# A decoder layer on one core: attention scores from float32r parts, whole-row moves of the values, expert rows by token

## The chip, the cores and the metric

The kernel runs on one core of a Trainium2 chip. It is one launch. The metric is the device time of that launch in microseconds (us). The kernel before takes 2743.19 us (median of three runs, 2734.66 to 2744.45). One further execution was profiled; its trace is what the text reads.

Five engines work side by side, each through its own queue in order: PE (TensorE, matrix products), DVE (VectorE), ACT (ScalarE), POOL (GpSimd) and SP (SyncE, which here issues every DMA). PEld is PE's loading of the stationary operand.

## The reference, cut to what matters

All is float32. There are B = 32 sequences of L = 256 tokens and D = 256 channels. Each passes three blocks, and each block ends in `x = layernorm(x + block(x))`:

```python
# 1. state-space block: d_inner 512, 16 states, chunks of 64 tokens
xc, res = split(x @ W_in.T + b_in); u = silu(causal_conv3(xc))
dlt, Bm, Cm = split(u @ W_x.T);     delta = softplus(dlt @ W_dt.T + b_dt)
h[t] = exp(delta[t] * A) * h[t-1] + delta[t] * Bm[t] * u[t]   # from zero in each chunk
y = sum_n(h * Cm) * silu(res);      block = y @ W_out.T + b_out
# 2. cross-attention: 16 heads of 16 channels, 256 keys from ctx
block = softmax(q @ k.T / 4) @ v  -> @ w_o.T + b_o
# 3. eight experts, FF = 704; tokens 32e .. 32e+31 of a sequence belong to expert e
block = (silu(x @ w1[e]) * (x @ w3[e])) @ w2[e]
```

## The kernel before, in words

**The state-space block** sets the rhythm. A step covers 32 of the 512 inner channels of one sequence, so there are 16 steps to a sequence and 512 in all (`STEPS`). In a step, SP loads delta and delta*u with every row repeated for eight states (`ld`), ACT takes four exponentials (`da`, L573), DVE makes `bu` (L602) and runs the recurrence as one scan over 1024 elements (L621), POOL multiplies by C (L637), and after every fourth step PE sums over the states (`y`, L651) and DVE gates the sum (`yg`, L667). The loads run three steps ahead (`AHEAD`). Both `bu` and B (`b_bc`) lie in PSUM.

**Attention** of a sequence follows its last step: the product with `w_out`, residual and layernorm, transposes, the product with `w_q` (`queries`, L789). Keys and values are made ahead (`keys_ahead`, L691) and kept in DRAM. Queries and keys go through DRAM as well, and come back by `spread_heads` (L678) with the 16 channels of a head at partitions 0 to 15 or 64 to 79 of `qT` and `kT`; the rest of these 64-row halves is zero. `scores` (L809) makes two heads at a time, one in each 64-row half: four float32 matmuls of 256 columns, a group. A head's scores are made twice. `maxima` (L825) makes them with queries along the partitions, and DVE reduces each head to its row maxima (`tops`, L838). The negative maxima are transposed on PE (L844), copied by ACT (L847), written to DRAM and loaded into row 63 and row 127 of `qT`; the same rows of `kT` are ones. `attns` (L874) then makes the scores with keys along the partitions, so that the maximum is already subtracted; ACT takes the exponentials (`es`, L894) and PE multiplies by the values (L863). Values lie as `v[P, 2, H, 32]`: 16 channels of a head, a one (for the sum of the softmax) and 15 zeros. They are loaded by two DMAs in pieces of 16 elements. `finish` (L924) divides, multiplies by `w_o` and applies the second layernorm; the result goes to DRAM (`x2d`).

**Experts** come in 32 units. The first 24 take 256 rows of one expert from eight sequences. The last eight, for sequences 24 to 31, take 128 rows of each of two experts from four sequences; four of them need sequence 31. A unit loads its rows (`load_xe`, L1070, through `rows_of`, L1065), transposes them, runs w1, w3 and w2 (L1133, L1197, L1212), adds and normalizes, and stores to `out`.

**The order of the work** is written by a planner at build time. Each part is a generator (a chain) that says when it could go on and on which engine; `in_order` (L80) always takes the chain that can start first, by a clock of assumed costs (`spend`; `MM`, `EV`, `VE`, `GP` from L307). It assumes that a DMA lands 3.5 us after its issue (`LANDING`). What a chain issues is then fixed in the engines' queues; on the chip every instruction waits for what it needs. PSUM gives five banks to all products (`RING`); `take` reserves banks and `done` returns them.

```python
        ss = [bank("s").rearrange("p (t n) -> p t n", t=2) for _ in heads]
        for t in range(2):
            for h, s in zip(heads, ss):
                g, r = h // 2, HR * (h % 2)
                nc.tensor.matmul(s[:, t, :], left[r : r + n, g, t * P : (t + 1) * P],
                                 right[r : r + n, g, :], start=True, stop=True)
        return ss, spend("PE", 2 * MM + 0.2)
```

## Time and profile before

| what | value |
|---|---|
| median of three runs | 2743.19 us |
| the profiled execution, its own time | 2743.78 us |
| its span, first to last instruction | 2742.0 us |
| first `bu` of the scans starts | 42.59 us |
| last scan ends | 2513.4 us |
| mean granted TensorE clock | 0.959 |
| DMA | 505.86 MB in 491497 packets, 177204 of them under 512 B |
| `v<-v_all` issue time on SP, min / median / max | 543 / 1177 / 3422 ns |

The profile's page gives the busy time of each engine, a row of tenths over 40 equal slices of the span, the DMA queues, the chain of work that ended last, and the costliest groups of instructions: line, engine, operation, `out<-in`, shapes, count, then busy time, mean duration in ns, idle time of the engine just before them and what ended it. A float32 matmul leaves two records, so 1024 matmuls appear as x2048. The view by windows gives the busy time of each engine in a stretch of the span. The view of waits tells which engine waited for which. The timeline tells the instructions in order, with the idle time before one and its releaser in brackets.

### The profile page before, as it was taken

The page shows a single profiled execution, that of the slowest core. Times are in us where ns is not written, and L with a number is a line of the kernel's source. Part 1 is how long each engine was busy: PE and PEld are TensorE (multiplying, and loading weights), DVE is VectorE, ACT ScalarE, POOL GpSimd, SP SyncE. Part 2 cuts the span into 40 slices and gives each one's busy share as a digit, 9 for nine tenths or more (in the row PEclk, how much of TensorE's full clock was granted, in tenths as well). Part 3 has the DMA queues.
Part 4 walks back from the last instruction along what each step waited for, and adds up shares of the span by engine and source line. Part 5 has one row for each costly group of instructions (what it writes and reads, how often), then busy time and mean ns, then how long its engine had stood idle before and what let it go on. Part 6 is the DMA issues. An engine that isn't in the chain of part 4 may idle for free.

```text
span 2742.0 us, 48659 instructions
## 1 busy us (share of the span) xinstructions
PE 2466.3 (90%) x16964; PEld 1705.3 (62%) x16964; DVE 2380.6 (87%) x2413; ACT 2043.4 (75%) x4327; POOL 1643.7 (60%) x1145
## 2 busy tenths in 40 slices
PE   5788989889899899989998989999999899998988
PEld 4565666566566666666666666665666566666767
DVE  4999999999999999999999999999999899896212
ACT  6887888888778878887878778888788788674331
POOL 4775766666666666575666665666666666553000
PEclk8899999999999999998999999999999999999999
DMA  7866666666676666676666666667666566666464
GB/s 203 228 199 176 193 187 181 189 191 191 187 199 186 181 167 190 176 197 177 167 198 187 198 175 186 187 177 195 190 197 179 163 172 180 185 174 181 150 195 144
DMA packets 491497, 505.86 MB, mean 184 GB/s; under 512 B 177204, under 2 KB 339252, under 8 KB 491252
## 3 DMA queue, kind: packets, MB, share of 16 engines
q1 hardware_dynamic: 491252, 502.75, 64.8%
q8 instruction: 135, 2.21, 0.4%
q14 instruction: 110, 0.90, 0.1%
HBM read 426.07 MB, written 76.55 MB: 183 GB/s over the span
## 4 chain that ended last, share of the span: by engine, by line
PE 29%; DVE 11%; ACT 8%; DMA 5%; issue 3%; POOL 1%; SPq 1%; DVEq 0%; ACTq 0%; POOLq 0%
PE ps_h L1133 8%; PE s L816 6%; DVE h L621 5%; PE ps_down L1212 4%; ACT da L573 3%; PE y L651 3%; DVE bu L602 2%; DVE tops L838 2%; PE ps_in L349 2%; PE ps_oT L863 2%; DMA ld<-dd 1%; DMA xe<-x2d 1%; PE ps_out L349 1%; PE ps_qk L349 1%; ACT es L894 1%
## 5 line engine op out<-in xcount | busy, mean ns | idle before, releaser
L637 POOL TENSOR_TENSOR h<-h,c_bc 128x1024 f32<-128x1024 f32 x512 | 1209.1, 2362 | 740.6 <-DVE h L621 627.0
L621 DVE TENSOR_TENSOR_SCAN h<-da,bu 128x1024 f32<-128x1024 f32 x512 | 1168.9, 2283 | 50.4 <-ACT da L573 5.8
L573 ACT ACTIVATE da<-ld,a_neg 128x252 f32<-128x252 f32 x2048 | 864.6, 504 | 188.3 <-DVE h L621 138.4
L602 DVE TENSOR_TENSOR bu<-ld,b_bc 128x1024 f32<-128x1024 f32 x512 | 626.1, 1223 | 19.9 <-DMA ld<-dd 8.0
L816 PE MATMUL s<-kT,qT 63*128 63x256 f32 x2048 | 345.4, 416 | 45.6 <-DVE tops L838 22.8
L894 ACT ACTIVATE es<-s 128x512 f32<-128x512 f32 x512 | 277.9, 594 | 140.6 <-PE s L816 75.9
L838 DVE TENSOR_REDUCE tops<-s 128x2 f32<-128x512 f32 x512 | 325.2, 677 | 41.6 <-PE s L816 41.1
L1133 PE MATMUL ps_h<-x2T,w 128*128 128x256 f32 (+2 forms) x1536 | 343.5, 368 | 9.5 <-ACT es L894 1.7
L816 PE MATMUL s<-qT,kT 64*128 64x256 f32 x2048 | 313.8, 405 | 22.5 <-DMA qT<-tops 13.0
L651 PE MATMUL y<-h,sel_y 128*32 128x256 f32 x4096 | 280.8, 397 | 52.3 <-POOL h L637 36.9
L816 PEld LDWEIGHTS s<-kT,qT 63*128 63x128 f32 x2048 | 213.8, 193 | 151.9 <-DVE tops L838 50.8
L1133 PEld LDWEIGHTS ps_h<-x2T,w 128*128 128x128 f32 (+1 forms) x1536 | 246.7, 186 | 89.7 <-issue 35.1
L349 PE MATMUL ps_in<-xT,w_in 128*128 128x256 f32 x1024 | 258.4, 397 | 8.7 <-ACT da L573 2.6
L816 PEld LDWEIGHTS s<-qT,kT 64*128 64x128 f32 x2048 | 200.9, 189 | 102.3 <-issue 39.6
L651 PEld LDWEIGHTS y<-h,sel_y 128*32 128x32 f32 x4096 | 131.8, 113 | 177.4 <-POOL h L637 55.1
L349 PEld LDWEIGHTS ps_in<-xT,w_in 128*128 128x128 f32 x1024 | 192.8, 196 | 60.4 <-issue 12.9
L420 POOL TENSOR_TENSOR u<-u,shifted 128x512 f32<-128x512 f32 x128 | 151.4, 1183 | 39.7 <-ACT u L407 34.7
L323 POOL TENSOR_SCALAR ln_rstd<-ln_mv 128x2 f32<-128x2 f32 x96 | 20.9, 218 | 254.2 <-DVE ln_mv L320 250.0
L407 ACT ACTIVATE shifted<-ps_in,tap_b,conv_w 128x256 f32<-128x256 f32 x256 | 130.8, 567 | 22.5 <-PE ps_in L349 10.9
L863 PE MATMUL ps_oT<-es,v 128*32 128x256 f32 x2048 | 142.4, 391 | 3.7 <-DVE h L1197 1.2
L349 PE MATMUL ps_out<-w_out,yg 128*128 128x256 f32 x512 | 117.6, 383 | 0.4 <-DVE yg L667 0.4
L375 ACT ACT_TABLE_LOAD x90 | 115.5, 1283 | 1.4
(135 smaller groups left out, 2987.5 us busy)
## 6 DMA issues: line engine op xcount, KB each, us to landing
ld<-dd SPq DMA_DIRECT2D x1024, 256.0 KB
w<-in_w SPq DMA_DIRECT2D x128, 352.0 KB
x<-in_x SPq DMA_DIRECT2D x64, 256.0 KB
dd<-delta SPq DMA_DIRECT2D x32, 512.0 KB
dd<-u SPq DMA_DIRECT2D x32, 512.0 KB
w<-in_w SPq DMA_DIRECT2D x32, 384.0 KB
w13y<-in_w SPq DMA_DIRECT2D x32, 352.0 KB
c_bc<-bcd SPq DMA_DIRECT2D x64, 128.0 KB
```

What stands on the lines that cost most here:

```text
L349: nc.tensor.matmul(ps[:, j, :], l, r, start=(k == 0), stop=(k == len(terms) - 1))
L420: nc.gpsimd.tensor_tensor(u[:, cc], u[:, cc], at, ALU.add)
L573: nc.scalar.activation(da[:, g, q].rearrange("p (k t) -> p k t", t=CHUNK)[:, :, 1:], loads[i][:, 0, g].rearrange("p (k t) -> p k t", t=CHU ...
L602: nc.vector.tensor_tensor(bu, loads[i][:, 1].unsqueeze(2).to_broadcast([P, GB, NQ, L]), b_bc.unsqueeze(1).to_broadcast([P, GB, NQ, L]), AL ...
L621: nc.vector.tensor_tensor_scan(h.rearrange("p g q t -> p (g q t)"), das_of.pop(i).rearrange("p g q t -> p (g q t)"), bu.rearrange("p g q t ...
L637: nc.gpsimd.tensor_tensor(hs[i], hs[i], c_bc, ALU.mult)
L651: nc.tensor.matmul(y[32 * j : 32 * j + 32, :], sel_y[:, g, :], hs[i - NJ + 1 + j][:, g, q, :], start=(g == 0 and q == 0), stop=(g == GB - ...
L816: nc.tensor.matmul(s[:, t, :], left[r : r + n, g, t * P : (t + 1) * P], right[r : r + n, g, :], start=True, stop=True,)
L838: nc.vector.tensor_reduce(top[:, h % 2, h // 2, :], s, AX.X, ALU.max)
L863: nc.tensor.matmul(oT[32 * j : 32 * j + 32, :], v[:, k, 4 * g + j, :], ess[j][:, k, :], start=(k == 0), stop=(k == 1), tile_position=(0, 3 ...
L894: nc.scalar.activation(es, s, AF.Exp, scale=1.0 / DK**0.5)
L1133: nc.tensor.matmul(ps[:m, i, :], w_tiles[u, which, e][k][:, f * P : f * P + m], right, start=(k == 0), stop=(k == 1),)
```

## The change

1. **Scores.** `qT` and `kT` become float32r. Queries and keys are split on POOL into a float32r copy (`hi`) and the rest (`lo = full - hi`): `parts_of`, two POOL instructions of 128x512 and two stores to DRAM for every sequence's queries and again for its keys. The 64 rows of a head now hold all four products: `qT` has (part, channel) with each row twice in a row, `kT` has (channel, part) and that twice over. `qT` comes by DMAs in which the repeat is an inner dimension of the source, 256 KB each in place of 64 KB, still four to a sequence; `kT` by eight DMAs of 128 KB in place of four of 64 KB.
2. **Maxima.** They don't go through DRAM any more. Two small POOL instructions split them into parts in `padded`, PE makes two 128x128 transposes in place of one, ACT writes the negative to `mTs`. In `attns`, each score matmul is followed by a second one that adds the maximum (`pick` picks the head's two rows): 1024 matmuls more.
3. **Values.** A row in DRAM holds 17 elements to a head, the ones with them, and `v` is loaded by one DMA of whole rows of 288 elements.
4. **Experts' rows.** `rows_of` puts the 32 tokens outside and the four sequences inside: the DMAs for `xe` and for `out` go from 4x32x256 to 32x4x256.
5. **Setup.** The weights and biases of q and k are put into the new column order by eight POOL copies; their bias loads are sixteen DMAs in place of eight.
6. **The planner's costs**: some are changed, and a group of scores is now put at 0.4 (maxima) or 0.7 in place of 1.14.

```diff
+F32R = mybir.dt.float32r
+DV = DK + 1
+VW = (H - 1) * DV + 32 + 1
-    k_all = dram.tile([B, D, L], F32, name="k_all")
-    v_all = dram.tile([B, L, D], F32, name="v_all")
+    k_all = dram.tile([B, DK, 2, 2 * NG, 2, L], F32, name="k_all")
+    v_all = dram.tile([B, L, VW], F32, name="v_all")
...
+        def ordered():
+            for k in range(2):
+                for i in range(2):
+                    at = slice(i * P, (i + 1) * P)
+                    nc.gpsimd.tensor_copy(
+                        w[:, k, at].rearrange("p (c j g) -> p g j c", j=2, c=DK),
+                        raw[:, k, at].rearrange("p (g j c) -> p g j c", j=2, c=DK),
+                    )
+            spend("POOL", 1.6)
...
-    kT = keep.tile([P, HG, L], F32, name="kT")
...
-    qT = keep.tile([P, HG, L], F32, name="qT")
-    nc.gpsimd.memset(qT, 0.0)
+    kT = keep.tile([P, HG, L], F32R, name="kT")
+    qT = keep.tile([P, HG, L], F32R, name="qT")
+    mTs = [keep.tile([P, L], F32R, name=f"mT_{i}") for i in range(2)]
+    padded = keep.tile([P, 2, 2, HR], F32R, name="padded")
+    pick = keep.tile([P, HG], F32R, name="pick")
...
-    MM = 0.47
-    EV = {1: 0.47, 2: 0.6, 4: 1.06}
-    VE = {1: 0.41, 2: 0.69, 4: 1.23}
-    GP = {1: 0.7, 2: 1.27, 4: 2.36}
+    MM = 0.49
+    EV = {1: 0.42, 2: 0.56, 4: 1.05}
+    VE = {1: 0.41, 2: 0.66, 4: 1.225}
+    GP = {1: 0.7, 2: 1.23, 4: 2.36}
...
+    def parts_of(n, b, full, t, d):
+
+        hi = unit1.tile([P, 2, L], F32R, tag="hi", name=f"{n}_hi_{b}")
+        lo = full.bitcast(F32R)
+        yield t, "POOL"
+        nc.gpsimd.tensor_copy(hi, full)
+        nc.gpsimd.tensor_tensor(lo, full, hi.bitcast(F32), ALU.subtract)
+        t = spend("POOL", 2 * GP[2])
+        yield t, "SP"
+        for s, part in enumerate((hi, lo)):
+            part = part.bitcast(F32)
+            if n == "q":
+                dma(d[:, s].rearrange("i c x t -> (c x) i t"), part)
+            else:
+                at = d[:, s].rearrange("c x i t -> c x (i t)")
+                dma(at, part.rearrange("p i t -> p (i t)"))
...
             for j in range(2):
-                src = d.rearrange("(i g j c) t -> i j c g t", i=2, j=2, c=DK)[half, j]
-                dma(dst[HR * j : HR * j + DK, 4 * half : 4 * half + 4, :], src)
+                at = dst[HR * j : HR * (j + 1), NG * half : NG * (half + 1), :].bitcast(F32)
+                if dst is qT:
+                    src = d[half, :, :, NG * j : NG * (j + 1)]
+                    src = src.rearrange("s c g t -> (s c) (g t)").unsqueeze(1)
+                    at = at.rearrange("p g t -> p (g t)")
+                    dma(at, src.to_broadcast([2 * DK, 2, NG * L]))
+                else:
+                    src = d[:, :, NG * j : NG * (j + 1), half].rearrange("c s g t -> (c s) g t")
+                    for s in range(2):
+                        dma(at[2 * DK * s : 2 * DK * (s + 1)], src)
...
-            for t in range(2):
-                src = v_all[b, t * P : (t + 1) * P].rearrange("p (h d) -> p h d", d=DK)
-                dma(v[:, t, :, :DK], src)
+            dma(v, v_all[b].rearrange("(t p) c -> p t c", p=P))
...
-    def scores(heads, left, right, n):
+    def scores(heads, left, right, lowered):
...
                 nc.tensor.matmul(
                     s[:, t, :],
-                    left[r : r + n, g, t * P : (t + 1) * P],
-                    right[r : r + n, g, :],
+                    left[r : r + HR, g, t * P : (t + 1) * P],
+                    right[r : r + HR, g, :],
                     start=True,
-                    stop=True,
+                    stop=not lowered,
                 )
-        return ss, spend("PE", 2 * MM + 0.2)
+            for h, s in zip(heads, ss):
+                g, r = h // 2, HR * (h % 2)
+                if lowered:
+                    nc.tensor.matmul(
+                        s[:, t, :],
+                        pick[r : r + HR, g : g + 1].to_broadcast([HR, P]),
+                        mTs[g // NG][r : r + HR, :],
+                        start=False,
+                        stop=True,
+                    )
+        return ss, spend("PE", 0.7 if lowered else 0.4)
...
-            nc.tensor.transpose(ps, top.rearrange("p j g t -> p (j g t)"), ident)
-            yield spend("PE", 0.2), "ACT"
-            rows = unit2.tile([H, P], F32, tag="rows", name="rows")
-            nc.scalar.activation(rows, ps, AF.Identity, scale=-1.0)
...
-            d = bcd.tile([2, 4 * L], F32, tag="tops", name="tops")
-            dma(d.rearrange("j (i n) -> (j i) n", n=P), rows)
-            yield clock.at["SP"] + LANDING, "SP"
-            dst = qT[HR - 1 :: HR, 4 * half : 4 * half + 4]
-            dma(dst.rearrange("j g t -> j (g t)"), d)
-            tts[b, half] = clock.at["SP"] + LANDING
+            nc.gpsimd.tensor_copy(hi, full)
+            nc.gpsimd.tensor_tensor(lo, full, hi.bitcast(F32), ALU.subtract)
...
+            for k in range(2):
+                src = padded[:, k].rearrange("p j r -> p (j r)").bitcast(F32)
+                nc.tensor.transpose(ps[:, k * P : (k + 1) * P], src, ident)
+            yield spend("PE", 0.6), "ACT"
+            nc.scalar.activation(mTs[half], ps, AF.Identity, scale=-1.0)
+            t = spend("ACT", EV[1])
             done(1, t)
+            tts[b, half] = t
...
-                    v[:, k, 4 * g + j, :],
+                    v[:, k, (4 * g + j) * DV : (4 * g + j) * DV + 32],
...
-                ss, ts = scores(range(h, h + 2), kT, qT, HR)
+                ss, ts = scores(range(h, h + 2), kT, qT, True)
...
-        return t[b : b + FOUR, CT * e : CT * (e + 1), :]
+        return t[b : b + FOUR, CT * e : CT * (e + 1), :].rearrange("b t d -> t b d")
```

## The prediction on record

> **What bounds the kernel now.** I read the page first, then windows cut at the first `bu` and at the end of the last scan, then DVE's waits in the long window, then PE's timeline.
>
> ```profile
> PE 2466.3 (90%) x16964; PEld 1705.3 (62%) x16964; DVE 2380.6 (87%) x2413; ACT 2043.4 (75%) x4327; POOL 1643.7 (60%) x1145
> ...
> PE   5788989889899899989998989999999899998988
> ...
> DVE  4999999999999999999999999999999899896212
> ```
>
> PE looks like the bound (90%), but DVE's row is all nines until the 35th slice and then falls away. So there are two regimes. The windows (columns: stretch, length, busy time of each engine, PE clock, DMA share, GB/s) put numbers to them:
>
> ```profile
> 42.60:2513.40 2470.80, 2243.28 (x15483) 1525.82 (x15481) 2320.03 (x2281) 1946.46 (x4149) 1605.88 (x1061) 0.96 0.66 186
> 2513.40:2742.00 228.60, 198.00 (x1399) 160.22 (x1397) 52.85 (x119) 71.03 (x133) 19.76 (x50) 0.93 0.54 172
> ```
>
> The span is 42.6 (start) + 2470.8 (main) + 228.6 (tail) = 2742.0 us; the execution's own time is 1.8 more, 2743.78, against a median of 2743.19. In main DVE is busy 94%, PE 91%. In the tail only PE is (87%). DVE's waits in main:
>
> ```profile
> DVE tops L838 <- PE s L816: 22.5, 26, 3.5
> DVE yg L667 <- PE y L651: 16.1, 14, 3.0
> DVE xe L1224 <- PE ps_down L1212: 13.0, 4, 6.9
> DVE x L964 <- PE ps_o L349: 10.2, 9, 2.6
> DVE bu L602 <- DMA ld<-dd: 8.0, 3, 6.3
> DVE h L621 <- ACT da L573: 5.8, 4, 2.6
> ```
>
> All rows of that view sum to 95.1 us, 78.2 of them ended by PE. DVE's idle time there is 2470.8 - 2320.0 = 150.8; the other 55.7 are gaps that no semaphore ends, mostly about 0.13 us between a `bu` and the scan that reads it. They stay. So without any wait main would still take 2470.8 - 95.1 = 2375.7 us. This is the key to the change: it frees PE, but in main PE can give back 78 us at most, and the rest has to come from the tail.
>
> **Part 1, scores on PE.**
>
> ```profile
> L816 PE MATMUL s<-kT,qT 63*128 63x256 f32 x2048 | 345.4, 416 | 45.6 <-DVE tops L838 22.8
> L816 PE MATMUL s<-qT,kT 64*128 64x256 f32 x2048 | 313.8, 405 | 22.5 <-DMA qT<-tops 13.0
> ```
>
> A group (two heads, four matmuls) is eight records. Undisturbed groups start 1.06 us before the next work (timeline: 2518.01 to 2519.07), 132 ns a record. Of 512 groups 488 are in main, 517 us. A float32r matmul isn't in the trace. Top end: it costs two records as now, and since a second matmul comes with each one in `attns`, 244 x 1.06 + 244 x 2.12 = 776, a loss of 259. Low end: the cheapest 256-column records here, `y`, 32 in about 1.87 us or 58 ns: 0.23 and 0.47 a group, 171 in all, a gain of 346. I take one record at 132 ns for each matmul, since shape and row halves are those of today's scores: 0.53 and 1.06, 388 us, a gain of 129. PE in main then goes from 2243 to about 2114 us, 87% of the shorter main (78% at the low end). Which of the two holds matters little, since both leave DVE as the bound. Of DVE's 78.2 us of PE waits I keep a third, 26 (bounds 0 and 78: in-order queues keep some order-made waits whatever the load). The other 16.9 us of waits stay.
>
> The changed kernel's order of instructions has one expert unit more before the last scan (24 of 32 in place of 23) and two `tops` more: +3 us of DVE after overlaps. Main: 2375.7 + 3 + 26 + 17 = 2422.
>
> **Part 2, POOL.** 128 instructions of 128x512 at 1.18 us (row L420) are 151 us, and 128 tiny ones at about 0.2 (rows L323, L326) 26. POOL goes from 1606 to about 1783 us in main, 74%. A multiplication by C comes later by a pair at most, 2.4 us; six `h` buffers cover it (the scan waited for POOL 1.0 us in all). Without that cover it would be 64 x 2.4 = 154 us. I take 0. In `maxima` the two tiny POOL instructions, two transposes and one ACT copy (some 2 us) replace a store and a load through DRAM (8.26 + 4.64 us where the chain shows them, 2528 to 2541).
>
> Would POOL's new reads slow DVE? The scan took 2253/2286/2290 ns (min, median, max) over 512 cases, while POOL was busy 65% of main; I charge nothing. [...]
>
> **Part 3, moves.** SP: v saves 64 issues of 1.18 us for 32 of about 0.5, tops' 128 issues of 0.46 go; 128 more kT issues of 0.42 and 64 stores of 0.5 come. Net about -30 us of SP, 0 on the path. DMA: qT and kT grow by 25 MB each, the parts' stores by 17, v by 2: +69 MB. At 186 GB/s for a share of 66% the queues move 282 GB/s when busy, so this is up to 245 us, 10 points of share, less what 131072 fewer 64-byte packets save. Main has the room on average; the price of bursts is a rival below. In the forecast, 0.
>
> Experts' rows: in the tail the first transposes after sequence 31 wait for one half, then for the next.
>
> ```profile
> 2644.93 0.30 PE L1118 MATMUL ps_xe<-ident,xe 128*128 128x128 f32 x1 [1.22 <-DMA xe<-x2d]
> 2646.75 0.55 PE L1118 MATMUL ps_xe<-ident,xe 128*128 128x128 f32 x3 [1.52 <-DMA xe<-x2d]
> 2649.08 0.45 PE L1118 MATMUL ps_xe<-ident,xe 128*128 128x128 f32 x1 [1.78 <-DMA xe<-x2d]
> 2650.80 0.90 PE L1118 MATMUL ps_xe<-ident,xe 128*128 128x128 f32 x3 [1.27 <-DMA xe<-x2d]
> ...
> 2702.70 5.75 PE L1133 MATMUL ps_h<-x2T,w13y 128*128 128x128 f32 x48
> ```
>
> With the 2.46 and 1.67 of the third unit and 1.97 earlier these are 11.9 us; bounds 0 and 12, I take 7. [...]
>
> **The tail.** After the last `y` PE has 704 matmuls in the old order and 613 in the new. Scores: 22 groups at 1.06 become 8 at 0.53 and 9 at 1.06, -9. One unit less there: 64 `ps_h` at 0.24 (5.75 for 24 matmuls), 12 `ps_down` at 0.46, 24 `ps_oT` at 0.13: -24. The round trip of tops: other products fill most of it, the idle parts left at 2531 to 2541 sum to 9, of which I count -5. Experts' rows -7. New on sequence 31's path: two POOL instructions, one more store and larger qT loads, +4. Tail: 228.6 - 41 = 188.
>
> **Start.** Eight more bias loads on SP at 0.59 us are 4.7; SP sat idle 4.1 us before `dd<-delta` at 33.14, so 0.6 to 1.5 remain; I take 1.5.
>
> **Sum.** 42.6 + 1.5 + 2422 + 188 + 1.8 = 2655.9; I say **2656 us**, -3.2%.
>
> **Rivals.**
> - *DVE's waits all go and the tail is denser*: main 2390, tail 172, 2608. For it: at PE's low end PE has 22% of slack. Against: in-order queues. Chance 0.10.
> - *The gain of main is lost to transfers.* qT's 512 KB for a half take 1.8 us at 282 GB/s, but 5.5 us if only the idle third (about 95 GB/s) serves them, against the 3.5 us on which the order was planned; PE waits up to 2 us at the head of its queue in each of 64 halves. With half of 128 us reaching DVE: 2656 + 60 = 2716. For it: the share rises to some 76%. Against: qT was waited for only 5.9 us. Chance 0.13.
> - *The change doesn't do what it says: slower.* float32r costs PE as much as float32. Then the added matmuls make PE the bound: main needs 2243 + 259 = 2502 of PE, at 96% use 2606, and the tail grows by 9 x 1.06 instead of falling by 9, about 207: 42.6 + 2606 + 207 + 2 = 2858. PE is the bound from about 180 us of added matmul time on (2243 + 180 = 2422, main's DVE time). For it: 63 and 64 rows cost today what 128 do, so nothing but fewer records can help. Chance 0.13, with other ways to be late in the same place.
> - Between, within 0.5%: 0.04. Forecast (2620 to 2700): 0.60.
>
> 0.5% is about what a measurement of this kernel can tell from no change. Faster by more: 0.60 + 0.10 + 0.13 = 0.83; same 0.04; slower 0.13. The range 2605 to 2730 takes the second rival and the first, and leaves the slower one out.
>
> **What would show it.** Right: `s` rows with half the records or less; PE in main under 88%; DVE's waits on PE near 26 us and DVE at 96% of main; main near 2422 and tail near 188; POOL 74%; no `tops<-rows`. Wrong: new DVE or PE waits on `qT<-heads` or `kT<-k_all`; scans that wait for POOL; `s` records that are as many as matmuls times two; a first `bu` later than 45.

## The result, and the profile after

The changed kernel is slower: 2780.88 us (median of 4 runs, 2777.42 to 2784.37) against 2743.82 for the kernel before beside it, a ratio of 1.0143 (95% interval 1.0119 to 1.0166). The forecast was 2656. The profiled execution takes 2777.42 us, its span is 2775.7.

The page of the changed kernel: busy times, then PE, DVE and the granted clock in 40 slices.

```profile
PE 2354.4 (85%) x16004; PEld 1644.8 (59%) x16004; DVE 2381.9 (86%) x2413; ACT 2063.1 (74%) x4331; POOL 1787.5 (64%) x1408
...
PE   6688888887898988898888988888779988888988
...
DVE  3988999999999998999998998899998999988422
...
PEclk8888898989899999999789999999888988988999
```

The same last row on the page of the kernel before, which the prediction did not show:

```profile
PEclk8899999999999999998999999999999999999999
```

PE has become emptier, as forecast, and DVE has eights where it had nines, which was not. What stands out is the clock that PE is granted (PEclk, in tenths of full speed): the mean over the span fell from 0.959 to 0.899, and all four runs of the changed kernel have 0.898 to 0.903. The windows (main, then tail; columns as before):

```profile
46.58:2590.04 2543.46, 2164.83 (x14760) 1491.43 (x14758) 2329.94 (x2295) 1974.14 (x4173) 1747.77 (x1315) 0.90 0.75 209
2590.04:2775.71 185.67, 158.91 (x1133) 129.65 (x1132) 46.35 (x106) 57.07 (x107) 21.17 (x52) 0.95 0.60 192
```

Start 46.6 (+4.0), main 2543.5 (+72.7, forecast 2422), tail 185.7 (-42.9, forecast 188). The loss is in main, with 4 us in the start; the order of the changed kernel also does one expert unit more before the last scan, as the prediction counted. DVE is busy in main for 2330 us, 10 more than before, and idle for 213.5, 63 more. Its waits in main:

```profile
DVE tops L897 <- PE s L865: 65.2, 48, 5.8
DVE yg L696 <- PE y L680: 26.8, 24, 3.1
DVE h L1258 <- PE ps_h L1194: 11.8, 6, 3.4
DVE xe L1285 <- PE ps_down L1273: 10.8, 6, 6.5
DVE rec L1001 <- PE ps_oB L996: 9.5, 6, 3.0
DVE bu L631 <- DMA ld<-dd: 8.2, 3, 6.3
```

Waits on PE have grown, the one on `s` from 22.5 to 65.2, although PE has less to do; all rows of this view that PE ended sum to 145 us, against 78 before. The scores themselves changed as hoped: one record to a matmul, and less busy time in three rows than the 659 us of two rows before (busy, mean ns; idle before).

```profile
L865 PE MATMUL s<-kT,qT 64*128 64x256 f32 x1024 | 184.8, 378 | 123.3 <-DVE tops L897 57.7 <-DMA qT<-heads 23.6 <-issue 15.4
L865 PE MATMUL s<-qT,kT 64*128 64x256 f32 x1024 | 195.7, 345 | 31.9 <-DVE tops L897 11.7 <-ACT es L955 8.6 <-DVE h_k_flat L1258 2.7
L875 PE MATMUL s<-mT,pick 64*128 64x256 f32 x1024 | 167.0, 308 | 3.4 <-ACT mT L914 3.4
L680 PE MATMUL y<-h,sel_y 128*32 128x256 f32 x4096 | 298.6, 414 | 37.6 <-POOL h L666 29.3 <-DVE tops L897 5.3 <-ACT x1T L832 1.6
```

The last row is work that the change does not touch: a `y` record takes 414 ns where it took 397. Its row in the kernel before:

```profile
L651 PE MATMUL y<-h,sel_y 128*32 128x256 f32 x4096 | 280.8, 397 | 52.3 <-POOL h L637 36.9 <-ACT es L894 7.6 <-ACT k_flat L355 3.7
```

How this goes together can be seen in one place of the changed kernel. PE's timeline (start, length, work, idle time before and its releaser), the windows of 3.4 us over it (the clock is the third number from the end), and DVE's timeline:

```profile
1331.63 0.38 PE L374 MATMUL ps_in<-xT,w_in 128*128 128x256 f32 x1
1334.97 0.35 PE L865 MATMUL s<-kT,qT 64*128 64x256 f32 x1 [2.96 <-ACT da L602]
1336.10 0.70 PE L865 MATMUL s<-kT,qT 64*128 64x256 f32 x7 [0.77 <-DMA qT<-heads]
1337.30 2.59 PE L865 MATMUL s<-kT,qT 64*128 64x256 f32 x8 [0.50 <-DVE tops L897]
1339.82 3.64 PE L680 MATMUL y<-h,sel_y 128*32 128x256 f32 x32
```

```profile
1333.70:1337.10 3.40, 1.05 (x8) 0.71 (x8) 3.27 (x3) 3.39 (x8) 3.40 (x3) 1.00 1.03 240
1337.10:1340.50 3.40, 3.16 (x16) 1.96 (x20) 3.40 (x7) 3.40 (x10) 3.40 (x3) 0.50 0.76 191
1340.50:1343.90 3.40, 3.40 (x30) 1.27 (x22) 2.44 (x5) 1.29 (x4) 1.79 (x4) 0.50 0.00 1
```

```profile
1336.58 4.85 DVE L897 TENSOR_REDUCE tops<-s 128x2 f32<-128x512 f32 x8
1341.35 1.22 DVE L631 TENSOR_TENSOR bu<-ld,b_bc 128x1024 f32<-128x1024 f32 x1
1343.53 0.42 DVE L696 TENSOR_TENSOR yg<-y,sres 128x256 f32<-128x256 f32 x1 [0.96 <-PE y L680]
1343.87 2.28 DVE L650 TENSOR_TENSOR_SCAN h<-da,bu 128x1024 f32<-128x1024 f32 x1
```

In the first window PE works 1.05 of 3.40 us, because it waits: behind ACT, then for a late `qT`, then for `tops` to free a bank. In the next two the clock is at 0.50. The 32 records of `y`, which took 1.93 us in an undisturbed place of the kernel before (at 2515.94), take 3.64 here; DVE waits 0.96 us for `y`, and comes to the next scan only after it.

### The profile page after: what moved, and what is told of

Same layout as the page of the kernel before. It is cut to its first block, busy times and chain, and to the rows that moved or that the text cites. A ratio compares the mean times of both kernels' runs of the same rounds, so it can differ in the third digit from the quotient of the medians.

```text
span 2775.7 us, 47073 instructions
## 1 busy us (share of the span) xinstructions
PE 2354.4 (85%) x16004; PEld 1644.8 (59%) x16004; DVE 2381.9 (86%) x2413; ACT 2063.1 (74%) x4331; POOL 1787.5 (64%) x1408
## 5 line engine op out<-in xcount | busy, mean ns | idle before, releaser
L1194 PE MATMUL ps_h<-x2T,w 128*128 128x256 f32 (+3 forms) x1632 | 390.9, 388 | 22.1 <-DVE x L1025 6.2
L897 DVE TENSOR_REDUCE tops<-s 128x2 f32<-128x512 f32 x512 | 323.3, 678 | 65.8 <-PE s L865 65.7
L1194 PEld LDWEIGHTS ps_h<-x2T,w 128*128 128x128 f32 (+1 forms) x1632 | 278.0, 199 | 106.0 <-issue 28.2
L374 PE MATMUL ps_in<-xT,w_in 128*128 128x256 f32 x1024 | 285.2, 429 | 43.3 <-ACT xT L414 33.6
L865 PE MATMUL s<-kT,qT 64*128 64x256 f32 x1024 | 184.8, 378 | 123.3 <-DVE tops L897 57.7
L865 PEld LDWEIGHTS s<-kT,qT 64*128 64x128 f32 x1024 | 114.7, 219 | 211.5 <-DVE tops L897 87.0
L865 PE MATMUL s<-qT,kT 64*128 64x256 f32 x1024 | 195.7, 345 | 31.9 <-DVE tops L897 11.7
L865 PEld LDWEIGHTS s<-qT,kT 64*128 64x128 f32 x1024 | 128.6, 206 | 102.4 <-issue 31.4
L924 PE MATMUL ps_oT<-es,v 128*32 128x256 f32 x2048 | 163.1, 422 | 9.5 <-DVE tops L897 4.7
L875 PE MATMUL s<-mT,pick 64*128 64x256 f32 x1024 | 167.0, 308 | 3.4 <-ACT mT L914 3.4
L875 PEld LDWEIGHTS s<-mT,pick 64*128 64x128 f32 x1024 | 124.8, 209 | 4.0 <-ACT mT L914 3.6
```

Source lines behind the costliest of these rows:

```text
L374: nc.tensor.matmul(ps[:, j, :], l, r, start=(k == 0), stop=(k == len(terms) - 1))
L865: nc.tensor.matmul(s[:, t, :], left[r : r + HR, g, t * P : (t + 1) * P], right[r : r + HR, g, :], start=True, stop=not lowered,)
L875: nc.tensor.matmul(s[:, t, :], pick[r : r + HR, g : g + 1].to_broadcast([HR, P]), mTs[g // NG][r : r + HR, :], start=False, stop=True,)
L897: nc.vector.tensor_reduce(top[:, h % 2, h // 2, :], s, AX.X, ALU.max)
L924: nc.tensor.matmul(oT[32 * j : 32 * j + 32, :], v[:, k, (4 * g + j) * DV : (4 * g + j) * DV + 32], ess[j][:, k, :], start=(k == 0), stop=( ...
L1194: nc.tensor.matmul(ps[:m, i, :], w_tiles[u, which, e][k][:, f * P : f * P + m], right, start=(k == 0), stop=(k == 1),)
```

## The experiments

Theories. **Clock**: with cheaper scores PE has more stretches in which it is mostly idle; after such a stretch the clock is granted at half ("half clock"), as in the place above; what PE does then takes about twice as long (the `y` there 3.64 us for 1.93), and DVE waits for it. **New waits**: the larger transfers, the POOL split and the `pick` matmuls cost DVE waits. **Order**: the planner's new prices give a worse order. **Work is work**: the clock has no part in it.

Ratios are to the kernel before in the same session, with 95% intervals; clocks are of the profiled run. "Single" is one float32r score matmul where a float32 one stood, with the low parts left out.

### Scores alone, in the old order

```diff
-    kT = keep.tile([P, HG, L], F32, name="kT")
-    qT = keep.tile([P, HG, L], F32, name="qT")
+    kT = keep.tile([P, HG, L], F32R, name="kT")
+    qT = keep.tile([P, HG, L], F32R, name="qT")
```

> The kernel before with nothing changed but the type of kT and qT: the scores' matmuls are float32r, one pass, on the same 63 and 64 rows, in the same order on every engine. It leaves out the low parts, so the scores have less precision. Theory 'clock': s records halve (1024 per line), PE has less to do, falls idle in more stretches, and the granted clock falls from 0.96 towards 0.92 or less; the other matmuls (y 397 ns, ps_in 397 ns) get slower by several per cent, DVE's waits on PE stay at half of before or more, and the time lies between 2690 and 2750 us. Rival 'new waits' (transfers, POOL's parts): none of those is here, so the gain forecast for the scores comes in full: DVE's waits on PE fall to a third, 2670 to 2690 us, clock 0.95 or more. Rival 'order': the same, 2670 to 2690, since the order is that of before.

2755.03 us, 1.0040 (1.0024 to 1.0056), clock 0.898. ("One pass" means one record to a matmul, as on the changed kernel's page above: x1024 for 1024 matmuls, where the kernel before has x2048.) No instruction was moved or added, and the time rose. Main:

```profile
44.00:2534.77 2490.77, 2085.09 (x13541) 1395.98 (x13539) 2319.82 (x2282) 1945.52 (x4150) 1606.59 (x1061) 0.90 0.65 185
```

Main is 20 us longer than before with the same DVE work, and DVE's waits on PE there went from 78 to 95 us. Clock and waits went as the clock theory said; the time lies 5 us above its range, and far from the 2670 to 2690 of the other two. Neither new transfers nor POOL's parts nor another order can act here; a cost of the float32r matmuls themselves still could.

### The same, doubled

```diff
+                for _ in range(2):
                     nc.tensor.matmul(s[:, t, :], left[...], right[...], start=True, stop=True)
```

> The float32r scores alone (the kernel before with kT and qT of type float32r, low parts left out), with each of the scores' matmuls issued twice into the same place: PE gets 2048 matmuls more, some 270 us of records, and gives the same result. Theory 'clock': the added matmuls put back the load on PE that the float32 scores had, the granted clock goes back from 0.90 to 0.94 to 0.96, y from 424 ns to about 400, and the time is no longer than that of the scores alone, 2735 to 2760 us. Rival 'work is work': the clock has no part in it and PE's work adds up; 270 us more, of which PE's idle time of 400 us in the main stretch can take a half: 2800 us or more.

2754.49 us, 1.0033 (1.0014 to 1.0053), clock 0.918. 2048 added matmuls cost nothing, so work is not simply work; but the clock came back only a third of the way (0.94 to 0.96 was expected) and the time not at all.

### The changed kernel with maxima doubled, and with the old price

```diff
+                for _ in range(1 if lowered else 2):
...
-        return ss, spend("PE", 0.7 if lowered else 0.4)
+        return ss, spend("PE", 2 * MM + 0.2)
```

The two edits are two kernels.

> The changed kernel with each matmul of maxima issued twice into the same place, 1024 more matmuls with the same result, order otherwise unchanged. Theory 'clock': the added work fills stretches in which PE waited for DVE's tops, the granted clock rises from 0.90 to 0.93 or more, the other matmuls get faster (y from 414 ns towards 397), and the time stays at 2781 or falls, to 2740 to 2780. Rivals 'new waits' and 'order': PE gets 65 to 130 us of work more and nothing in return: 2790 to 2840 us.

2792.03 us, 1.0172 (1.0147 to 1.0197), clock 0.921. This went against the clock theory: the clock rose, but not to the 0.93 expected, and the time lies in the range of its rivals (2790 to 2840). DVE's wait for `s` grew from 65 to 78 us. The added load in `maxima` stands straight in front of DVE's `tops`, which may be why; no run tested that.

> The changed kernel with one number of the planner put back: a group of scores is priced at 1.18 us, nearly the price before, in place of 0.4 and 0.7; no instruction is added or taken away, only the order changes. Rival 'order': PE's queue is no longer filled with scores that stand and wait for DVE, DVE's waits on PE fall by half and the time to 2690 to 2740 us. Theory 'clock': the price changes only which work stands in the queue; PE's total is the same, the clock stays between 0.89 and 0.92, and the time within 1% of 2781.

2781.54 us, 1.0144 (1.0117 to 1.0172), clock 0.902. Main is 46 us shorter and the tail 59 longer: work was moved, nothing won. The price is not the cause.

### The two smaller parts alone

Values in whole rows and the experts' rows, as in the change, in the kernel before; then the same with `spend("SP", ISSUE)` added, so that PE's and DVE's orders stay as they were; then the experts' rows only.

```diff
-        return t[b : b + FOUR, CT * e : CT * (e + 1), :]
+        return t[b : b + FOUR, CT * e : CT * (e + 1), :].rearrange("b t d -> t b d")
```

> The kernel before with the two smaller parts of the change alone: values in whole rows with their ones, and the experts' rows as outer dimension. The scores are those of before. All theories: the wait of the first transposes after sequence 31 for their rows goes from 11.9 us to 5 or less, the main stretch stays within 10 us, and the time is 2730 to 2745 us. A loss here would mean that these parts, and not the scores, make the changed kernel slower.

2719.35 us, 0.9907 (0.9874 to 0.9940), clock 0.965: these parts are no loss, and gain more than the range expected.

> The kernel before with values in whole rows and the experts' rows as outer dimension, but the planner is told that v still takes two transfers' issue, so that PE's and DVE's orders are word for word those of before. The kernel with the same moves and its own order took 0.991 of before. If the moves themselves bring this, 0.989 to 0.993 here too, 2712 to 2724 us; if the other order brings it, the rows' 7 to 12 us remain: 2731 to 2740.

2707.42 us, 0.9865 (0.9845 to 0.9886), clock 0.966. The moves bring it; the planner's other order seems to take some back, though the two intervals touch.

> The kernel before with only the experts' rows as outer dimension, order as before. By the sum of the prediction 7 us, by its bounds 0 to 12: 2731 to 2743 us.

2715.56 us, 0.9897 (0.9880 to 0.9913), clock 0.965: 28 us (22 between the profiled runs), more than the bound of 12. The first transposes of the units (kernel before, then this one):

```profile
L1118 PE MATMUL ps_xe<-ident,xe 128*128 128x128 f32 x128 | 24.3, 305 | 20.9 <-DMA xe<-x2d 19.3 <-ACT u L407 1.6
```

```profile
L1118 PE MATMUL ps_xe<-ident,xe 128*128 128x128 f32 x128 | 22.0, 293 | 6.6 <-DMA xe<-x2d 4.8 <-ACT u L407 1.6
```

The tail became 11.5 us shorter, inside the step's bounds. Main became 12.2 us shorter too, where the step had counted nothing; DVE's waits on PE in main fell with it, from 78.2 to 65.7 us.

### What the changed kernel adds

Half of the bytes in the loads of `kT` and `qT`; no split on POOL; no second matmul in `attns`; and the three together.

```diff
-                    dma(at, src.to_broadcast([2 * DK, 2, NG * L]))
+                    dma(at[: 2 * DK].unsqueeze(1), src)
...
-        nc.gpsimd.tensor_copy(hi, full)
-        nc.gpsimd.tensor_tensor(lo, full, hi.bitcast(F32), ALU.subtract)
...
-                if lowered:
+                if False:
```

> The changed kernel with as many DMAs as it has, but the loads of kT and qT bring half the rows (one copy of each part, the other rows stay zero), some 33 MB less in all; it leaves out the products of high with low parts. Theory 'clock': the transfers cost little, the time stays between 2765 and 2785 us and the clock at 0.90. Rival 'new waits': the 256 KB loads are what makes PE wait for qT (23.6 us) and delays ld; that wait goes below 8 us and the time falls to 2730 to 2760.

2750.06 us, 1.0028 (1.0007 to 1.0050), clock 0.903: 31 us less than the changed kernel. PE's wait for `qT` there, after the one in the changed kernel, and the loads' median landing (last number, us) in the same order:

```profile
PE s L865 <- DMA qT<-heads: 23.6, 23, 4.3
```

```profile
PE s L867 <- DMA qT<-heads: 7.7, 10, 2.6
```

```profile
qT<-heads SPq DMA_DIRECT2D x128, 256.0 KB, 6.2
```

```profile
qT<-heads SPq DMA_DIRECT2D x128, 128.0 KB, 4.8
```

DVE's wait for `s` fell with it, from 65.2 to 41.3 us, in a profiled run that is 13 us above the median. The time lies in the range of "new waits" and outside that of the clock theory: the transfers were a real cost, as the rival of the prediction had it.

> The changed kernel without the two POOL instructions that split q and k: both parts are stored from the same tile, so the low part is left out (the high one is counted twice). 128 POOL instructions of 1.2 us go, some 155 us, and q's and k's stores come 2.5 us earlier. Theory 'clock': POOL had slack, 2765 to 2785 us. Rival 'new waits': q's path and POOL's queue cost DVE waits; 2735 to 2760.

2774.31 us, 1.0111 (1.0072 to 1.0149), clock 0.901.

> The changed kernel without the second matmul of attns, so that the row maxima are not subtracted before the exponential; all else, the order too, as it is. PE loses 1024 records, 167 us of busy time. Theory 'clock': PE is idle in yet more stretches, the clock falls from 0.90 to 0.87 or 0.88, and of the 167 us no more than 40 reach the end: 2740 to 2775 us. Rival 'work is work': the pick matmuls are what makes the changed kernel 25 us longer than the float32r scores alone; without them DVE's PE waits fall by half, 2690 to 2730 us, at a clock of 0.90.

2772.63 us, 1.0112 (1.0075 to 1.0150), clock 0.899. Each is some 8 us below the changed kernel, and both intervals overlap its own, so neither the 155 us of POOL nor the 167 of PE can be told from no cost. The clock did not fall further, against what was expected.

> The changed kernel with three of its additions gone at once: half the bytes of the kT and qT loads, no POOL split (the stored parts are equal), no second matmul in attns (maxima not subtracted); it leaves out the low parts and the cross products. What stays is one-pass scores in the changed kernel's own order with both moves. If the rest of the loss is the sum of these three (31, 7 and 8 us one by one), 2725 to 2745 us, the 2747 of the float32r scores with the moves, at a clock of 0.90. If it is above 2760, the order that the planner makes with the new prices costs time by itself.

2743.39 us, 1.0003 (0.9982 to 1.0024), clock 0.899: 38 us less than the changed kernel. What is left is single scores with the moves in the changed kernel's order; the next kernel has the same in an order made with the old prices, and takes 2747. The new order costs nothing that can be seen.

### Moves and float32r scores, with the load put back in steps

All in the order of the kernel with the two moves, so that its float32 scores (2719 us) are the point to compare with. First one matmul for each score:

> The kernel with the two moves (2719 us) and float32r scores besides, low parts left out, in exactly the same order. Theory 'clock': again nothing comes of the freed 250 us of PE: the clock falls from 0.965 to 0.90 and the time is that of the moves alone or up to 20 us more, 2715 to 2740. Rival 'work is work': here the order is another one, with less stalls on DVE, and PE's gain arrives: 2660 to 2700, clock 0.95.

2746.93 us, 1.0017 (1.0006 to 1.0027), clock 0.889. Same order, some 320 us of PE's work less (512 groups at 0.624 us, the difference of the prices found below), and 28 us longer: worse than the clock theory's range. DVE's waits on PE in main went from 60 to 98 us. Then each matmul four times; four times but single in the last sequence; three times but single in the last sequence:

```diff
-                nc.tensor.matmul(...)
+                for _ in range(3 if b < B - 1 else 1):
+                    nc.tensor.matmul(...)
```

> The kernel with both moves and float32r scores (2747 us at a clock of 0.889) with each of the scores' matmuls issued four times into the same place: 6144 matmuls more, which add nothing to the result, in the same order. PE's load in the scores is again about that of the float32 scores. Theory 'clock': the clock goes back to 0.95 or more and the time falls, although only work was added, to 2715 to 2738 us. Rival 'float32r itself' (a change between kinds of matmul, or the one-pass form, costs time whatever the load): 2747 or more, as the cause is still there fourfold.

2747.54 us, 1.0013 (1.0000 to 1.0026), clock 0.960. The clock came back, main fell by 16 us, the tail grew by 17. So a cost of float32r itself is not ruled out by this run.

> As the fourfold kernel (both moves, float32r scores, low parts left out, each of the scores' matmuls issued four times), but single for the last sequence, whose scores lie in the tail where PE sets the time. Theory 'clock': the main stretch is that of the fourfold kernel (2465 us, clock 0.96) and the tail that of the single one (219 us, in place of 236): 43 + 2465 + 219 + 2 = 2729 us, 18 less than either of the two (2747). Rival 'the clock only goes with it': more matmuls never make it faster; 2747 or more, as both ends were.

2740.84 us, 0.9994 (0.9978 to 1.0010), clock 0.955: less than single, but 12 us over what was expected.

> The same with three in place of four: 4064 added matmuls. Theory 'clock': the load is a little under that of the float32 scores, the clock 0.93 to 0.95, main between 2450 and 2475, 2715 to 2738 us. Rival 'the clock only goes with it': 2747 or more.

2722.82 us, 0.9932 (0.9909 to 0.9955), clock 0.942: **24 us faster than the single one, with 3968 matmuls added** that give nothing. (The 4064 of the expectation is a miscount; 31 sequences at 2 x 64 make 3968.) Main of the float32 kernel with the moves, then of the single, the threefold and the fourfold one with the single tail:

```profile
42.78:2485.25 2442.47, 2222.94 (x15383) 1513.21 (x15382) 2312.04 (x2268) 1946.69 (x4143) 1605.34 (x1060) 0.97 0.64 189
```

```profile
43.41:2524.06 2480.65, 2091.60 (x13456) 1401.09 (x13454) 2314.13 (x2268) 1946.48 (x4145) 1605.35 (x1060) 0.88 0.63 186
```

```profile
43.70:2504.85 2461.15, 2206.08 (x17317) 1592.23 (x17315) 2312.24 (x2268) 1948.00 (x4144) 1608.58 (x1060) 0.94 0.63 187
```

```profile
43.18:2516.69 2473.51, 2296.41 (x19245) 1713.95 (x19244) 2316.08 (x2268) 1946.21 (x4143) 1609.64 (x1060) 0.96 0.63 186
```

DVE's work is the same in all four. From single to threefold PE gets more work, the clock rises from 0.88 to 0.94, DVE's waits on PE fall from 98 to 81 us, and main is 19 us shorter. With fourfold PE is busy 93% of main, the clock, at 0.96, has little left to give, and main is longer again in this profile; the kernel with four everywhere had 2464.7 with the same main, so single profiles differ here by some 9 us, while the medians, 2740.84 against 2722.82, are clear of each other. A cost that each float32r matmul brings cannot make threefold faster than single. What remains argued is that the added load helps through the clock alone, and not also by the moments at which PE comes to its other work.

### The clock by itself

PE does n matmuls, waits for one reduction on VectorE, and so on; each of the two kernels ran once. In the first such kernel the runs of 32 matmuls that were to part the stretches had been moved into the waits, so its stretches tell nothing by themselves.

> A kernel by itself that computes nothing of the reference: 18 stretches of some 60 us, in each of which PE does n matmuls and then waits for one VectorE reduction of their result, again and again, so that PE's busy share is about constant in a stretch. Three kinds of matmul: float32 on 128 rows (n = 1, 2, 3, 4, 6, 10), float32 on 64 rows, two side by side (2, 4, 6, 8, 12, 16), float32r on 64 rows (4, 8, 12, 16, 24, 40). A run of 32 float32 matmuls stands ahead of each. Theory 'clock': in stretches with PE busy under about 60% the granted clock is 0.5 all along, over 85% it is 1.0, between them it changes back and forth; the kind of matmul shifts the point by no more than 15 points. Rival: the clock does not follow PE's load, and is 0.9 to 1.0 in all stretches.

> The kernel by itself once more, with its order of instructions held: 32 float32 matmuls, then some 70 us in which PE does n matmuls and waits for one VectorE reduction, and so on for 18 stretches (float32 on 128 rows, n = 1, 2, 3, 4, 6, 10; float32 on 64 rows, 2, 4, 6, 8, 12, 16; float32r on 64 rows, 4, 8, 12, 16, 24, 40). It computes nothing of the reference. Theory 'clock': the stretches in which PE is busy under about 60% run at a granted clock of 0.5, those over 85% at 1.0. Rival: the clock is 0.9 or more in all of them, or follows the kind of matmul and not the busy share.

Windows inside four stretches, each after its first 7 us (columns: PE, PEld, DVE, POOL, clock, DMA share, GB/s): float32r n = 16 and 24, float32 on 64 rows n = 4 and 6.

```profile
1191.60:1244.71 53.11, 38.87 (x305) 33.35 (x301) 12.46 (x18) 0.00 (x0) 0.50 0.00 1
1266.90:1298.88 31.98, 22.08 (x313) 19.50 (x313) 8.69 (x13) 0.00 (x0) 1.00 0.01 1
```

```profile
591.20:667.35 76.15, 55.52 (x217) 31.53 (x213) 17.99 (x26) 0.00 (x0) 0.50 0.00 0
689.79:738.60 48.81, 32.88 (x253) 22.66 (x253) 13.85 (x21) 0.00 (x0) 1.00 0.00 1
```

After their first microseconds the stretches are half or full: of ten such windows four have a clock of 1.00, five 0.50 and one 0.51. The period of the repetition (reduction to reduction, median) gives the price of a matmul: at full clock 3447 ns with n = 40 and 2487 with 24, so 60 ns for a float32r matmul; 4517 and 2358 with n = 16 and 6, so 216 ns for a float32 one on 64 rows. At half clock it is 107 (1585 with n = 4, 2867 with 16) and 426 (2020 with 2, 2872 with 4). A float32 matmul on 128 rows takes 431 (3642 with 6, 5367 with 10). What is not matmul is 1.05 us of a period. So at full clock the matmuls would fill, by an estimate from these numbers, 48% of the period of n = 16 (0.96 of 2.01 us), and that stretch fell to half; with 24 they fill 58%, and it stayed full. For float32 on 64 rows the two are 45% (half) and 55% (full); on 128 rows 29% (half, n = 1) and 45% (full, n = 2). The theory was right that the clock follows PE's load; its limits of 60 and 85% were the author's estimate, and too high by this measure. The busy share of the trace does not serve here, since a matmul at half clock is busy for longer: the first window above is 73% busy (38.87 of 53.11 us) at half clock, the second 69% at full. No gap is long: PE's timeline in the stretches of n = 16 and n = 24,

```profile
1231.17 2.08 PE L72 MATMUL pass<-r 64*128 64x256 f32 x16 [0.79 <-DVE top L93]
1234.03 2.08 PE L72 MATMUL pass<-r 64*128 64x256 f32 x16 [0.79 <-DVE top L93]
```

```profile
1282.26 1.70 PE L72 MATMUL pass<-r 64*128 64x256 f32 x24 [0.79 <-DVE top L93]
```

shows the same 0.79 us at a time in both, at half clock in the first and at full clock in the second.

### Float32r where PE has no pause

The fastest kernel so far (the moves in the old order, 2707 us) with float32r scores for sequence 31 alone, which lie in the tail:

```diff
+                if b < B - 1:
+                    lt, rt = lt.bitcast(F32), rt.bitcast(F32)
```

> The fastest so far (both moves in the old order, float32 scores, 2707 us), with float32r scores for the last sequence only, low parts left out there; order unchanged. In the tail PE works without a break, so the freed time should arrive: 16 groups at some 0.24 in place of 0.86 us, 10 us. Theory 'clock': 2695 to 2703 us with the clock as it was, 0.96 to 0.97. Rival 'float32r gains nothing anywhere': 2707.

2697.62 us, 0.9843 (0.9818 to 0.9867), clock 0.971. The tails of the two kernels, float32 first:

```profile
2487.65:2702.51 214.86, 195.62 (x1399) 157.97 (x1397) 52.74 (x119) 70.92 (x133) 19.76 (x50) 0.96 0.56 183
```

```profile
2486.78:2694.39 207.61, 187.31 (x1335) 152.27 (x1333) 52.38 (x119) 70.82 (x133) 19.76 (x50) 0.96 0.58 189
```

The same change of type that lost 28 us over the whole kernel (there in the planner's own order) took 7 us off the tail. The two totals' intervals touch, so the tail is the evidence, and one pair of tails is not enough: with the same work in them, those of the single, threefold and fourfold kernels above were 219.5, 222.3 and 226.9 us. But it shortened in both other pairs too: 228.6 to 217.8 for the scores alone, 230.4 to 219.5 with the moves. This kernel is faster than both, but lacks the low parts in one sequence; with the full computation the best is the one before it, 0.9865.

## Why the prediction was wrong, point by point

In shares of the time before, the result is a sum of four: the moves -0.93%, single scores +1.10% (1.0017 less 0.9907), the new order -0.14% (inside the intervals), and the transfers, the split and `pick` together +1.40% (1.0143 less 1.0003). That makes +1.43.

- **What bounds the kernel: right.** DVE sets main, PE the tail. (DVE's row falls away after its 36th slice, with an eight at the 32nd, not at the 35th; nothing rests on it.)
- **"One record at 132 ns for each matmul": wrong, the truth lay near the low end.** A matmul costs 60 ns (at full clock in the kernel by itself), so a group in `maxima` 0.24 us and not 0.53 (in the changed kernel's tail 0.42 from its start to the next work's, at 2637.22, where a group took 1.06 before). "63 and 64 rows cost today what 128 do" was wrong too: 216 ns against 431, although a record lasts about as long (416 and 405 ns for the two rows of `s` before, 397 for `ps_in` on 128 rows). Records overlap (the eight of a float32 group, 405 ns each in the mean, start within 1.06 us), so neither their durations nor their number are prices: a float32 matmul has two records for one, and costs 3.6 times as much. A float32 group is 0.864 us by these prices, so in main of the changed kernel 244 x 0.624 + 244 x 0.384 (with the added matmuls) = 246 us of PE's work were freed, where 129 were forecast.
- **"A third, 26" of DVE's waits on PE: the step that failed.** They did not fall from 78 us to 26, they rose to 145 (the first five rows of the waits shown above are 124 of them). That is 119 of the 121 us by which main missed its 2422; DVE's own work was 7 us more than counted, and its other waits 5 less. With the scores alone the waits already stood at 95. The step took PE's speed as given. In main of the scores alone, PE's busy time should have fallen by 488 x 0.624 = 305 us and fell by 158; other records became longer (`y` 397 to 424 ns). The next two tables were taken from the traces: PE in the clock's own windows (the clock's records, 76 before and 186 after, begin and end on a grid of 3.413 us), and DVE's gaps of over 0.25 us by the clock during the gap.

| PE busy in a full-clock window | before: windows, next at half | after | moves, single scores |
|---|---|---|---|
| under 50% | 40, 32 | 62, 55 | 66, 62 |
| 50 to 65% | 31, 3 | 45, 24 | 55, 27 |
| 65 to 80% | 56, 3 | 75, 14 | 64, 8 |
| over 80% | 607, 0 | 464, 0 | 437, 0 |

| kernel | main at half clock | DVE gaps, us | of these at half clock | gaps' share of half-clock time | of full-clock time |
|---|---|---|---|---|---|
| before | 7.3% | 85.8 | 21.3 | 11.7% | 2.8% |
| after | 20.9% | 148.8 | 68.3 | 12.8% | 4.0% |
| scores alone | 20.4% | 107.2 | 46.2 | 9.1% | 3.1% |
| moves, float32 | 6.9% | 67.1 | 15.1 | 9.0% | 2.3% |
| moves, single | 23.4% | 104.5 | 50.8 | 8.8% | 2.8% |
| moves, threefold | 11.8% | 86.1 | 35.2 | 12.1% | 2.3% |

No window with PE over 80% busy was followed by half clock, in any of these three. (The windows of the first table cover the whole span, starts and tails included.) DVE stalls three to five times as much at half clock as at full, and the change nearly triples the time at half clock. (The table alone does not say which brings which; the threefold kernel, where load was the only thing added, does.) A second thing is in the last column: at full clock the stalls did not fall either. The waits that remained look like waits not for a share of PE but for its turn: work that comes late to PE from POOL, ACT or DVE, in a fixed order. No run separates these.
- **"No cost" for POOL, right; "in the forecast, 0" for transfers, wrong.** POOL's split was worth some 8 us and not to be told from none. The transfers were worth 31 us; the rival's mechanism (late `qT` at the head of PE's queue) was right: 23.6 us of PE's waiting in place of the 128 that it put, but more than that hung on it. The share of the DMA engines rose by 9 points in main, where 10 were put as the most.
- **Experts' rows -7: the term was too small,** 28 us by itself, 11.5 in the tail and 12.2 in main. The waits of `ps_xe` that the step counted in the tail had like ones in main; the whole list was 19.3 us and only the 11.9 of the tail were looked at. The 7 was the author's choice between the bounds; no run shows the term or its reason. What the runs showed in its place is the 28 us, with PE's waits for `xe` down from 19.3 to 4.8.
- **Tail 188: right in its total,** 185.7, **but partly by luck.** The 17 groups of scores left there (8 at 0.42 and 9 at 0.58 us, for 0.53 and 1.06) saved some 5 us more than counted, and PE still waited 13.3 us for `xe` (11.9 before), where the sum left 4.9. Most of it is one wait:

```profile
2690.37 0.48 PE L1179 MATMUL ps_xe<-ident,xe 128*128 128x128 f32 x1 [9.56 <-DMA xe<-x2d]
```
- **Start +1.5: too small,** +4.0.
- **Rivals.** None named the clock. The slower side was given 0.13 for PE becoming the bound by dear float32r; it was cheap, and the kernel became slower all the same.

A long pause is not needed for half clock here: in the repetition with n = 16 the gap between matmuls was 0.79 us each time and the clock was 0.50 all along, and with n = 24 the same gap stood at 1.00. What differed between the two is how much of the time matmuls fill (48 and 58% by the estimate above), not the length of a gap.

**Left open:** why doubling in `maxima` alone made the changed kernel 11 us slower, and doubling all of the scores alone won nothing, though the clock rose in both; whether the 28 us between float32 and single scores are the clock's to the last (the threefold kernel gives back 24 of them); and what in main the experts' rows shorten.

## What to carry to other kernels

Before a matmul is made cheaper in a kernel that another engine bounds, look at the clock row and at windows of 3.4 us: where PE is already busy under some 65% of a window, cheaper matmuls can buy half clock for the work behind them (in the changed kernel 79 of 107 such windows were followed by half clock, 14 of 75 at 65 to 80%, none of 464 above). Make them cheaper where PE runs without a pause (7 us off the tail here), and leave them dear, or fill the pause, where it waits (24 us from the threefold matmuls). Here the waits that were read from queues in a fixed order did not shrink with PE's load (78 us became 145, while PE's busy time in main went from 2243 to 2165); count such a wait as kept unless its releaser itself becomes earlier.

## What was not expected of the hardware

- In the traces of before and after the granted clock has two values, 1.0 and 0.5, and changes on a grid of 3.413 us. In the kernel by itself a matmul at half clock took nearly twice as long (60 to 107 ns, 216 to 426).
- The clock halved there without any long pause: with gaps of 0.79 us, when matmuls on 64 rows would fill 45 to 48% of the time at full clock (estimate), and stayed full at 55 to 58%. Two matmuls on 128 rows at 45% kept it full, so the share alone is not the rule.
- A float32r matmul of 256 columns on 64 rows, two side by side, cost 60 ns there, a float32 one 216, although the trace shows one record for the first and two for the second.
- 3968 matmuls with no use made a kernel 24 us faster (2746.93 to 2722.82).
